# Decays two units ahead, rows one unit ahead, and TensorE in order of emission in the last image

## The chip, the cores and the metric

One core of one Trainium2 chip runs the whole program in one launch. The metric is device time in microseconds, and lower is better. The notes speak of the engines by the profile's names: PE is TensorE (PEld its weight loads), DVE is VectorE, ACT is ScalarE, POOL is GpSimd and SP is SyncE, which here only issues DMAs.

## The reference

The input is four images of 128 x 128 pixels and 128 channels, float32. Two residual layers follow each other, each behind a group norm:

```
x = x + deformable_conv(group_norm(x))      # layer 0: learned offsets, bilinear samples, 3x3 depthwise, pointwise
x = x + mamba(group_norm(x))                # layer 1: two blocks, each row of an image is a sequence of 128 steps
```

A mamba block projects each row to 256 channels `u` and 256 gates, runs a short causal convolution and SiLU on `u`, derives a step size `delta = softplus(...)` and 16 pairs of `B` and `C` per time step, and then runs, for each of the 256 channels and 16 states,

```
h[t] = exp(delta[t] * A) * h[t-1] + delta[t] * u[t] * B[t];   y[t] = sum over states of h[t] * C[t]
```

The sum, plus `u * D`, is gated with SiLU and projected back to 128 channels.

## The kernel before

**Two layers side by side.** `layer0(b)` is a generator over the 288 sampling steps of image `b`: POOL gathers table rows by indirect DMA (L370), DVE or ACT weights them (`gw`, L398 and L393), PE transposes and adds them (`p`) and multiplies with the weights (`acc`, L427). `layer1` is a generator over the mamba work. Image 0 passes layer 0 alone. After that, `layer0(b + 1)` and the mamba blocks of image `b` are stepped against each other, and the last image has the mamba work alone.

**Jobs and units.** A job is a block of four rows and one of the two mamba blocks: 64 jobs an image, 256 in all, ordered in pairs of blocks, so that the next job never needs this job's output. A job has eight units (`q` from 0 to 7) of two states each (`NQ = 2`). In the first three images a unit is:

- the decays: a small copy (L655) and four `Exp` on ACT (L660) into one of three buffers `da` (`NDA = 3`);
- the rows of `B` and `C`, spread over the partitions by DMA (`bc`, L650);
- on DVE two products `hs = du * B` (L694), one long scan (L700) and the product with `C` (L703);
- the sums: 16 transposing matmuls on PE that add `da` to `y` (through the helper, L137).

In the last image (`in_last`) `B` is multiplied in before a transpose. `turn_du` turns `du` on PE (`pdu`, L531) and ACT copies it (`duts`, L532). A unit's scans then take their input from PSUM: POOL (first state, L679) and ACT (second state, L677) scale `duts` to `xs`, PE transposes `xs` to four tiles `px` (16 transposes, L684), DVE runs four scans of 512 steps (L686) and one product (L689). The `px` tiles of each state share two PSUM buffers, so a transpose for the next unit can start when the scan of this unit that used the same buffer is done.

**The projections of the next job.** `pre` is a generator that is stepped once after each unit of the running job: `pu` (L554), SiLU (L564), gates `pr` (L569), `pdb` (L578) and the transposes `pbt` (L588), `pdt` (L600), the softplus on ACT (L603 to L615, with `Exp` and `Ln` from different function tables), and then `delta`: in the first three images summed on PE (`pdl`, L621) and copied by ACT (`de`, L622), in the last image on DVE (`e`, `de`, L611 to L613). The product `du` (L624) closes it. At a job's end DVE gates `y` (`g`, L710), PE transposes it (`pyg`, L715), ACT copies (`yg`, L716), PE projects (`pout`, L720 or L727 and L729), and the next job opens `y` with 8 matmuls against the diagonal of `D` (L639).

**What sets the order.** A list scheduler orders each engine's instructions when the program is built: whatever it holds ready goes out, the one emitted earlier first, by its own idea of the durations. On the chip each engine works its list from the top, so the list is fixed before the run. In the kernel before, a unit emits in this order: rows, decays, `xs` and `px`, scans, product, sums; then the piece of `pre`.

Of the kernel before, what the change touches and what calls it, by code (L numbers as in the profile page):

```python
# [10 lines left out]
F32 = mybir.dt.float32  # L11
I32 = mybir.dt.int32
AF = mybir.ActivationFunctionType
ALU = mybir.AluOpType
# [3 lines left out]
P = 128  # L18
# [46 lines left out]
def block_kernel(ctx: ExitStack, tc: tile.TileContext, a: dict, out: bass.AP):  # L65
# [69 lines left out]
    def add_transposed(o, v, start, stop):  # L135

        nc.tensor.matmul(o, v, ident, is_transpose=True, start=start, stop=stop, skip_group_check=True)  # L137
# [375 lines left out]
    def in_last(blk):  # L513

        return blk * SR // H == B - 1
# [19 lines left out]
    def pre(st, l):  # L535
# [68 lines left out]
            nc.scalar.activation(de[:, c], pdt, AF.Relu)  # L604
        nc.scalar.activation(e, e, AF.Exp, scale=-1.0)
        nc.scalar.activation(w1, e, AF.Identity, bias=1.0)
        nc.scalar.activation(du, w1, AF.Ln)
        if in_last(blk):
            nc.scalar.activation(w1, w1, AF.Identity, bias=-1.0)
            yield  # L610
            nc.vector.tensor_tensor(e, w1, e, ALU.subtract)  # L611
            nc.vector.tensor_tensor(de, de, e, ALU.subtract)
            nc.vector.tensor_tensor(de, de, du, ALU.add)  # L613
        else:
            nc.scalar.activation(w1, w1, AF.Identity, scale=-1.0, bias=1.0)  # L615
            yield
            yield
            for c in range(NC):
                pdl = now["ps1"].tile([P, TB], F32, tag="t", name=f"pdl_{nm}_{c}")
                for k, v in enumerate((e, w1, du, de)):  # L620
                    nc.tensor.matmul(pdl, ident, v[:, c], start=(k == 0), stop=(k == 3))  # L621
                nc.scalar.copy(de[:, c], pdl)  # L622
            yield
        nc.vector.tensor_tensor(du, de, u, ALU.mult)  # L624
        st.update(u=u, g=g, delta=de, du=du, bcd=bcd)
# [2 lines left out]
            yield  # L628
            turn_du(st, nm)

    def main(st, l):

        blk = st["blk"]
        nm = f"{blk}_{l}"

        y = now["psy"].tile([P, SR, NC, P], F32, tag="y", name=f"y_{nm}")
        for i in range(SR):
            for c in range(NC):
                nc.tensor.matmul(  # L639
                    y[:, i, c], st["u"][:, c, i * P : (i + 1) * P], ddiag[:, l, c, :],  # L640
                    start=(i % 2 == 0 and c == 0), stop=False, skip_group_check=True,
                )
        if in_last(blk) and "dut" not in st:
            turn_du(st, nm)
        for q in range(NS // NQ):
            bc = []
            for w in range(in_last(blk), 2):
                t = lm[0].tile([P, NQ, TB], F32, tag=f"bc{w}", name=f"bc{w}_{nm}_{q}", bufs=2)
                n0 = w * NS + q * NQ
                nc.sync.dma_start(t, st["bcd"][n0 : n0 + NQ, :].partition_broadcast(P))  # L650
                bc.append(t)
            da = das[n_da[0] % NDA]
            n_da[0] += 1

            nc.scalar.copy(da.rearrange("p c n s t -> p (c n s) t")[:, :, 0], zero)  # L655
            for c in range(NC):
                dv = st["delta"][:, c].rearrange("p (s t) -> p s t", s=SR)
                for n in range(NQ):
                    s = q * NQ + n
                    nc.scalar.activation(  # L660
                        da[:, c, n, :, 1:], dv[:, :, 1:], AF.Exp, scale=aneg[:, l, c, s : s + 1]
                    )
            dc = da.rearrange("p c n s t -> p c (n s t)")
            cv = bc[-1].rearrange("p n t -> p (n t)").unsqueeze(1).to_broadcast([P, NC, NQ * TB])
            if in_last(blk):


                for n in range(NQ):
                    s = q * NQ + n

                    xs = lm[0].tile(
                        [P, SR, NC * P], F32, tag="bc0" if n else "gw", name=f"xs_{nm}_{s}", bufs=2
                    )
                    for i in range(SR):
                        bv = st["bt"][:, i, s : s + 1]
                        if n:
                            nc.scalar.activation(xs[:, i], st["dut"][:, i], AF.Copy, scale=bv)  # L677
                        else:
                            nc.gpsimd.tensor_scalar(xs[:, i], st["dut"][:, i], bv, None, ALU.mult)  # L679
                    for c in range(NC):  # L680
                        pool, tag = (now["ps"], "t") if n else (psa, "acc")
                        px = pool.tile([P, SR, P], F32, tag=tag, name=f"px_{nm}_{s}_{c}")
                        for i in range(SR):
                            nc.tensor.transpose(px[:, i, :], xs[:, i, c * P : (c + 1) * P], ident)  # L684
                        dn = da[:, c, n].rearrange("p s t -> p (s t)")
                        nc.vector.tensor_tensor_scan(  # L686
                            dn, dn, px.rearrange("p s t -> p (s t)"), 0.0, ALU.mult, ALU.add
                        )
                nc.vector.tensor_tensor(dc, dc, cv, ALU.mult)  # L689
            else:  # L690
                hs = lm[0].tile([P, NC, NQ, TB], F32, tag="hs", name=f"hs_{nm}_{q}")

                for n in range(NQ):
                    nc.vector.scalar_tensor_tensor(  # L694
                        hs[:, :, n, :], st["du"], one,
                        bc[0][:, n].unsqueeze(1).to_broadcast([P, NC, TB]),
                        op0=ALU.mult, op1=ALU.mult,
                    )
                df = da.rearrange("p c n s t -> p (c n s t)")
                nc.vector.tensor_tensor_scan(  # L700
                    df, df, hs.rearrange("p c n t -> p (c n t)"), 0.0, ALU.mult, ALU.add
                )
                nc.vector.scalar_tensor_tensor(dc, dc, one, cv, op0=ALU.mult, op1=ALU.mult)  # L703
            for c in range(NC):
                for n in range(NQ):
                    for i in range(SR):
                        add_transposed(y[:, i, c], da[:, c, n, i, :], False, q == NS // NQ - 1 and n == NQ - 1)
            yield
        gt = st["g"]
        nc.vector.tensor_tensor(gt, y.rearrange("p s c d -> p s (c d)"), gt, ALU.mult)  # L710
        yg = lm[0].tile([P, NC, TB], F32, tag="yg", name=f"yg_{nm}")
        for c in range(NC):
            pt = now["ps1"].tile([P, SR, P], F32, tag="t", name=f"pyg_{nm}_{c}")
            for i in range(SR):
                nc.tensor.transpose(pt[:, i, :], gt[:, i, c * P : (c + 1) * P], ident)  # L715
            nc.scalar.copy(yg[:, c], pt.rearrange("p s t -> p (s t)"))  # L716
        po = now["ps1"].tile([P, TB], F32, tag="t", name=f"pout_{nm}")
        if l < NL - 1:
            for c in range(NC):
                nc.tensor.matmul(po, ow[:, l, c, :], yg[:, c], start=(c == 0), stop=(c == NC - 1))  # L720
            st["h"] = next_h()
            nc.scalar.copy(st["h"][:, :, DCONV - 1 :], po.rearrange("p (s t) -> p s t", s=SR))
        else:
            x1t = load_x1(blk, f"o{nm}")
            for i in range(SR):
                o = po[:, i * P : (i + 1) * P]
                nc.tensor.matmul(o, x1t[:, i * P : (i + 1) * P], ident, start=True, stop=False)  # L727
                for c in range(NC):
                    nc.tensor.matmul(  # L729
                        o, yg[:, c, i * P : (i + 1) * P], ow[:, l, c, :], start=False, stop=(c == NC - 1)  # L730
                    )
            ot = lm[0].tile([P, NC, TB], F32, tag="w1", name=f"ot_{nm}")[:, 0].rearrange("p (r c) -> p r c", r=SR)
            nc.scalar.copy(ot.rearrange("p r c -> p (r c)"), po)
            b, row = divmod(blk * SR, H)
            nc.sync.dma_start(out[b, row : row + SR].rearrange("r w c -> w r c"), ot)
# [4 lines left out]
    for i in range(0, NB, 2):  # L740
        sts = [{"blk": blk} for blk in range(i, min(i + 2, NB))]
        jobs += [(st, l) for l in range(NL) for st in sts]

    def layer1():
        open_main()
        for _ in pre(*jobs[0]):
            pass
        for i, job in enumerate(jobs):

            nxt = pre(*jobs[i + 1]) if i + 1 < len(jobs) else iter(())  # L750
            for _ in main(*job):
                next(nxt, None)
                yield
            for _ in nxt:
                pass

    for j in range(NJ):
        stats_part(0, j)
# [98 lines left out]
```

## Time and profile before

| | |
|---|---|
| median of three runs | 24469.56 us (24467.03 to 24477.43) |
| the profiled execution: its time, its span | 24467.72 us, 24465.9 us |
| granted TensorE clock, mean | 0.928 |
| busy over the span: PE, DVE, ACT, POOL | 84%, 84%, 65%, 74% |
| stretch 5000 to 19500 us: DVE, PE, ACT, POOL busy of 14500 us | 13598, 12719, 10324, 11689 us |
| stretch 20149 to 24450 us: DVE, PE, ACT, POOL busy of 4301 us | 3801, 3441, 3461, 2345 us |

The span falls into three parts: layer 0 of the first image alone (to about 3100 us), the three images in which both layers run side by side (to about 20100 us), and the last image, whose 64 jobs run from the first scan at 20149 us to the last at 24450 us. A profile row of a group has the line, the engine, the operation, what it writes and reads, the shape and the count; then the busy time, the mean of one, and the idle time of the engine just before these instructions with what ended it. A row of the waits has the time in total, how often, and the longest.

### The profile page before, as it was taken

What the parts mean: (1) busy time and instruction counts of PE and PEld (TensorE: products, weight loads), DVE (VectorE), ACT (ScalarE), POOL (GpSimd) and SP (SyncE); (2) the same over time, 40 slices, a digit from 0 to 9 for tenths busy, and PEclk for the clock granted to TensorE, in tenths of its full rate; (3) what the DMA queues carried; (4) which work ended last, traced back from release to release, by engine and by line L of the source; (5) the groups of instructions that cost most, each with busy time, mean ns of one, the idle gap of its engine ahead of it and who ended that gap; (6) DMA issues with size and microseconds to landing.
All of it is one profiled execution on the core that took longest, in us unless ns stands there. A gap on an engine that the chain in (4) does not pass through costs nothing. (4 is left out here: it accounts for less than half of the span.)

```text
span 24465.9 us, 304806 instructions
## 1 busy us (share of the span) xinstructions
PE 20571.8 (84%) x109348; PEld 12814.4 (52%) x109348; DVE 20647.2 (84%) x12769; ACT 15875.8 (65%) x36074; POOL 18054.1 (74%) x11270
## 2 busy tenths in 40 slices
PE   5777788888888888888888888888988878777777
PEld 3444445555555555555555555555555546666666
DVE  3332369999999999999999999999999998888888
ACT  1111147777777767777777766777777768888887
POOL 4777778888888857888888857888888845555555
PEclk7888889999999999999999999999999989999999
DMA  5554544554545544554555544455545532222221
GB/s 150 155 157 125 149 132 160 162 162 163 163 161 165 162 148 161 162 162 162 162 164 163 163 148 159 163 161 163 164 162 164 162 126 69 70 70 70 69 70 68
DMA packets 1530702, 3470.14 MB, mean 142 GB/s; under 512 B 243283, under 2 KB 717651, under 8 KB 1529052
## 3 DMA queue, kind: packets, MB, share of 16 engines
q1 hardware_dynamic: 1086812, 2242.08, 28.5%
q0 software_dynamic: 442368, 1208.55, 15.5%
q8 instruction: 859, 14.07, 0.2%
q14 instruction: 663, 5.43, 0.1%
HBM read 3299.19 MB, written 150.47 MB: 141 GB/s over the span
## 5 line engine op out<-in xcount | busy, mean ns | idle before, releaser
L370 POOL DMA_INDIRECT gt<-table,idx x9216 | 15702.9, 1704 | 4130.4 <-issue 2793.6
L700 DVE TENSOR_TENSOR_SCAN da<-da,hs 128x2048 f32<-128x2048 f32 x1536 | 6792.7, 4422 | 810.7 <-ACT da L660 708.2
L660 ACT ACTIVATE da<-de,aneg 128x508 f32<-128x508 f32 x8192 | 5450.1, 711 | 1447.6 <-PE y L137 1313.8
L427 PE MATMUL acc<-s,wc 128*64 128x512 f32 (+2 forms) x23520 | 5854.9, 609 | 143.0 <-ACT s L416 136.1
L137 PE MATMUL y<-ident,da 128*128 128x128 f32 x32768 | 4410.3, 291 | 1187.1 <-DVE da L703 911.6
L137 PEld LDWEIGHTS y<-ident,da 128*128 128x128 f32 x32768 | 3936.2, 150 | 2099.3 <-DVE da L703 1028.3
L679 POOL TENSOR_SCALAR xs<-duts,bt 128x256 f32<-128x256 f32 x2048 | 2350.4, 1164 | 2249.6 <-ACT duts L532 1190.4
L694 DVE SCALAR_TENSOR_TENSOR hs<-du,misc,bc 128x1024 f32<-128x1024 f32 x3072 | 3829.4, 1283 | 0.2
L137 PE MATMUL p<-ident,gw 128*128 128x128 f32 x18432 | 2592.6, 293 | 1375.2 <-DVE gw L398 1359.0
L427 PEld LDWEIGHTS acc<-s,wc 128*64 128x64 f32 (+1 forms) x23520 | 1940.7, 141 | 3368.5 <-issue 2999.7
L703 DVE SCALAR_TENSOR_TENSOR da<-da,misc,bc 128x2048 f32<-128x2048 f32 x1536 | 3609.3, 2350 | 39.0
L398 DVE TENSOR_TENSOR gw<-gt,wt 128x1024 f32<-128x1024 f32 x1440 | 1756.1, 1220 | 2219.3 <-DMA gt<-table,idx 2010.2
L393 ACT ACTIVATE gw<-gt,wt 128x64 f32<-128x64 f32 x13824 | 3487.9, 337 | 93.0 <-DMA gt<-table,idx 86.0
L137 PEld LDWEIGHTS p<-ident,gw 128*128 128x128 f32 x18432 | 2247.6, 151 | 1972.1 <-DVE gw L398 1513.7
L686 DVE TENSOR_TENSOR_SCAN da<-da,px 128x512 f32<-128x512 f32 x2048 | 2350.4, 1202 | 506.6 <-PE px L684 506.6
L416 ACT COPY s<-p 128x512 f32<-128x512 f32 x1152 | 671.3, 583 | 2332.7 <-PE p L137 2330.6
L554 PE MATMUL pu<-hp,inc 128*128 128x512 f32 x4096 | 1823.0, 593 | 0.2 <-ACT duts L532 0.2
L684 PE MATMUL px<-ident,xs 128*128 128x128 f32 x8192 | 1210.6, 287 | 542.9 <-DVE da L686 328.2
L684 PEld LDWEIGHTS px<-ident,xs 128*128 128x128 f32 x8192 | 968.5, 147 | 824.1 <-POOL xs L679 331.0
L413 ACT COPY s<-halo 128x256 f32<-128x256 f32 x1116 | 433.4, 401 | 1220.4 <-PE acc L427 1218.4
L689 DVE TENSOR_TENSOR da<-da,bc 128x2048 f32<-128x2048 f32 x512 | 1172.2, 2290 | 6.5
L554 PEld LDWEIGHTS pu<-hp,inc 128*128 128x128 f32 x4096 | 746.9, 189 | 821.1 <-issue 820.4
(148 smaller groups left out, 17815.0 us busy)
## 6 DMA issues: line engine op xcount, KB each, us to landing
bc<-bcd SPq DMA_DIRECT2D x3584, 512.0 KB
gt<-table,idx POOLq DMA_INDIRECT x9216
table<-xg SPq DMA_DIRECT2D x1016, 64.0 KB
xt<-in_x SPq DMA_DIRECT2D x124, 320.0 KB
xr<-in_x SPq DMA_DIRECT2D x128, 256.0 KB
x<-xo SPq DMA_DIRECT2D x128, 256.0 KB
x1t<-x SPq DMA_DIRECT2D x128, 256.0 KB
x1t_o<-x SPq DMA_DIRECT2D x128, 256.0 KB
```

The lines of the kernel that those rows point to most:

```text
L137: nc.tensor.matmul(o, v, ident, is_transpose=True, start=start, stop=stop, skip_group_check=True)
L370: nc.gpsimd.indirect_dma_start(out=gt[:, v, r], out_offset=None, in_=flat, in_offset=bass.IndirectOffsetOnAxis(ap=idx[:, ri, o : o + 1], a ...
L393: nc.scalar.activation(gw[:, r, s, v], gts[h][:, v, r, s * CG : (s + 1) * CG], AF.Copy, scale=wt[:, u, r0 + r, s, v : v + 1],)
L427: nc.tensor.matmul(accs[b, j][CG * g : CG * g + CG, q, :], wc[sl, v, e, :], st[p + 4 * g if p < 4 else 8][sl, ky + q.start : ky + q.stop, ...
L554: nc.tensor.matmul(px.rearrange("p (s t) -> p s t", s=SR), inc[:, l, j, c * P : (c + 1) * P], h[:, :, j : j + P], start=(j == 0), stop=(j ...
L660: nc.scalar.activation(da[:, c, n, :, 1:], dv[:, :, 1:], AF.Exp, scale=aneg[:, l, c, s : s + 1])
L679: nc.gpsimd.tensor_scalar(xs[:, i], st["dut"][:, i], bv, None, ALU.mult)
L684: nc.tensor.transpose(px[:, i, :], xs[:, i, c * P : (c + 1) * P], ident)
L686: nc.vector.tensor_tensor_scan(dn, dn, px.rearrange("p s t -> p (s t)"), 0.0, ALU.mult, ALU.add)
L694: nc.vector.scalar_tensor_tensor(hs[:, :, n, :], st["du"], one, bc[0][:, n].unsqueeze(1).to_broadcast([P, NC, TB]), op0=ALU.mult, op1=ALU. ...
L700: nc.vector.tensor_tensor_scan(df, df, hs.rearrange("p c n t -> p (c n t)"), 0.0, ALU.mult, ALU.add)
L703: nc.vector.scalar_tensor_tensor(dc, dc, one, cv, op0=ALU.mult, op1=ALU.mult)
```

## The change

The decays leave the unit: a new function `decays` takes the next entry of a list `queue` of all units of all jobs. Two entries are made before the first unit, and each unit emits, behind its own product, the decays of the unit two later. A new function `head` emits the rows, the `xs` and the `px` of a unit; it is called one unit ahead, in between the decays and the sums. For the last unit of a job the rest of `pre` and the head of the next job's first unit take this place (`after`). In the first three images the softplus gets one more stop ahead of `Ln`, and `delta` is published as soon as it is copied. From the first job of the last image on, PE's instructions are kept in the order of emission (`manual_schedule`); the other engines stay with the scheduler.

```
         nc.scalar.activation(w1, e, AF.Identity, bias=1.0)
+        if not in_last(blk):
+            yield
         nc.scalar.activation(du, w1, AF.Ln)
...
                 nc.scalar.copy(de[:, c], pdl)
+            st["delta"] = de
             yield
...
+    def decays(st, l, q):
+        da = das[n_da[0] % NDA]
+        n_da[0] += 1
+        nc.scalar.copy(da.rearrange("p c n s t -> p (c n s) t")[:, :, 0], zero)
...
+        made.append(da)
+
+    def head(st, l, q):
...
+        return bc, pxs
+
+    def main(st, l, first, after):
...
+        ahead = first
         for q in range(NS // NQ):
+            bc, pxs = ahead
+            da = made.pop(0)
...
+            last = q == NS // NQ - 1
+            for f in queue[:1]:
+                decays(*queue.pop(0))
+            ahead = after() if last else head(st, l, q + 1)
             for c in range(NC):
                 for n in range(NQ):
                     for i in range(SR):
-                        add_transposed(y[:, i, c], da[:, c, n, i, :], False, q == NS // NQ - 1 and n == NQ - 1)
-            yield
+                        add_transposed(y[:, i, c], da[:, c, n, i, :], False, last and n == NQ - 1)
+            if not last:
+                yield
         gt = st["g"]
...
+    queue = [(st, l, q) for st, l in jobs for q in range(NS // NQ)]
+    made = []
     def layer1():
         open_main()
         for _ in pre(*jobs[0]):
             pass
+        for _ in range(NDA - 1):
+            decays(*queue.pop(0))
+        firsts = {0: head(*jobs[0], 0)}
         for i, job in enumerate(jobs):
+            if i and in_last(job[0]["blk"]) and not in_last(jobs[i - 1][0]["blk"]):
+                ctx.enter_context(tc.manual_schedule(engines={mybir.EngineType.PE}))
             nxt = pre(*jobs[i + 1]) if i + 1 < len(jobs) else iter(())
-            for _ in main(*job):
+            def after(i=i, nxt=nxt):
+                for _ in nxt:
+                    pass
+                if i + 1 < len(jobs):
+                    firsts[i + 1] = head(*jobs[i + 1], 0)
+            for _ in main(*job, firsts.pop(i), after):
                 next(nxt, None)
                 yield
-            for _ in nxt:
-                pass
+            yield
```

More of the change, by code (lines that the diff above doesn't have):

```diff
@@ L629, in pre @@
             turn_du(st, nm)
-    def main(st, l):
+    def decays(st, l, q):
+        da = das[n_da[0] % NDA]
+        n_da[0] += 1
+        nc.scalar.copy(da.rearrange("p c n s t -> p (c n s) t")[:, :, 0], zero)
+        for c in range(NC):
+            dv = st["delta"][:, c].rearrange("p (s t) -> p s t", s=SR)
+            for n in range(NQ):
+                s = q * NQ + n
+                nc.scalar.activation(
+                    da[:, c, n, :, 1:], dv[:, :, 1:], AF.Exp, scale=aneg[:, l, c, s : s + 1]
+                )
+        made.append(da)
+    def head(st, l, q):
+        blk = st["blk"]
+        nm = f"{blk}_{l}"
+        if in_last(blk) and "dut" not in st:
+            turn_du(st, nm)
+        bc = []
+        for w in range(in_last(blk), 2):
+            t = lm[0].tile([P, NQ, TB], F32, tag=f"bc{w}", name=f"bc{w}_{nm}_{q}", bufs=2)
+            n0 = w * NS + q * NQ
+            nc.sync.dma_start(t, st["bcd"][n0 : n0 + NQ, :].partition_broadcast(P))
+            bc.append(t)
+        pxs = {}
+        if in_last(blk):
+            for n in range(NQ):
+                s = q * NQ + n
+                xs = lm[0].tile(
+                    [P, SR, NC * P], F32, tag="bc0" if n else "gw", name=f"xs_{nm}_{s}", bufs=2
+                )
+                for i in range(SR):
+                    bv = st["bt"][:, i, s : s + 1]
+                    if n:
+                        nc.scalar.activation(xs[:, i], st["dut"][:, i], AF.Copy, scale=bv)
+                    else:
+                        nc.gpsimd.tensor_scalar(xs[:, i], st["dut"][:, i], bv, None, ALU.mult)
+                for c in range(NC):
+                    pool, tag = (now["ps"], "t") if n else (psa, "acc")
+                    px = pool.tile([P, SR, P], F32, tag=tag, name=f"px_{nm}_{s}_{c}")
+                    for i in range(SR):
+                        nc.tensor.transpose(px[:, i, :], xs[:, i, c * P : (c + 1) * P], ident)
+                    pxs[n, c] = px
+        return bc, pxs
+    def main(st, l, first, after):
         blk = st["blk"]
@@ L642, in main @@
                 )
-        if in_last(blk) and "dut" not in st:
-            turn_du(st, nm)
+        ahead = first
         for q in range(NS // NQ):
[L646 to L662, printed above, removed]
+            bc, pxs = ahead
+            da = made.pop(0)
             dc = da.rearrange("p c n s t -> p c (n s t)")
@@ L668, in main @@
                 for n in range(NQ):
[L669 to L679, printed above, removed]
                     for c in range(NC):
[L681 to L684, printed above, removed]
                         dn = da[:, c, n].rearrange("p s t -> p (s t)")
                         nc.vector.tensor_tensor_scan(
-                            dn, dn, px.rearrange("p s t -> p (s t)"), 0.0, ALU.mult, ALU.add
+                            dn, dn, pxs[n, c].rearrange("p s t -> p (s t)"), 0.0, ALU.mult, ALU.add
                         )
```

## The prediction

> **What bounds the kernel now.** I read the page first (the tenths of busy time, then the groups), then busy time by stage, then DVE's waits in the two stages that the change touches, then the timeline of one job of the last image. The page:
>
> ```profile
> DVE  3332369999999999999999999999999998888888
> ...
> L700 DVE TENSOR_TENSOR_SCAN da<-da,hs 128x2048 f32<-128x2048 f32 x1536 | 6792.7, 4422 | 810.7 <-ACT da L660 708.2
> ```
>
> DVE is at nine tenths or more while both layers run, and near it in the last image; its scans (L700) waited 708.2 us for decays. By stage (length, then busy time of PE, PEld, DVE, ACT, POOL):
>
> ```profile
> 5000.00:19500.00 14500.00, 12718.79 (x65682) 7585.34 (x65680) 13598.40 (x7273) 10324.29 (x25068) 11688.75 (x6044) 0.95 0.50 161
> 20149.00:24450.00 4301.00, 3441.46 (x21515) 2679.45 (x21513) 3801.08 (x2875) 3460.74 (x6192) 2345.20 (x2043) 0.94 0.21 70
> ```
>
> DVE is idle for 902 us in the first and 500 us in the second, so its idle time is what can be won. Its waits in the first stage (total, times, longest):
>
> ```profile
> DVE da L700 <- ACT da L660: 614.5, 135, 12.4
> DVE gw L398 <- DMA gt<-table,idx: 64.7, 18, 7.2
> ```
>
> And in the last image:
>
> ```profile
> DVE da L686 <- PE px L684: 506.6, 145, 13.4
> ```
>
> The waits for decays all lie at q = 4, 5 and 6, where ACT has the softplus, the sampling products and two table loads in its list. Of the 507 us in the last image 456 lie at one place, the second scan of q = 2. The timeline shows a job boundary there, and a chain to remember:
>
> ```profile
> 22109.08 1.20 DVE L710 TENSOR_TENSOR g<-y,g 128x1024 f32<-128x1024 f32 x1
> ...
> 22113.48 1.50 PE L639 MATMUL y<-ddiag,u 128*128 128x128 f32 x12
> ...
> 22116.57 3.60 PE L554 MATMUL pu<-hp,inc 128*128 128x512 f32 x8
> ...
> 22125.89 3.44 DVE L686 TENSOR_TENSOR_SCAN da<-da,px 128x512 f32<-128x512 f32 x3 [6.67 <-PE px L684]
> ```
>
> PE works through two `pu` of 3.6 us and two sets of sums, and only then the next `px`: 6.67 us of idle DVE, once a job. The second chain:
>
> ```profile
> 22160.02 1.20 DVE L624 TENSOR_TENSOR du<-de,u 128x1024 f32<-128x1024 f32 x1
> ...
> 22161.97 1.07 ACT L532 COPY duts<-pdu 128x512 f32<-128x512 f32 x2 [0.41 <-PE pdu L531]
> 22162.72 9.77 POOL L679 TENSOR_SCALAR xs<-duts,bt 128x256 f32<-128x256 f32 x8 [13.94 <-ACT duts L532]
> ...
> 22168.30 1.22 DVE L686 TENSOR_TENSOR_SCAN da<-da,px 128x512 f32<-128x512 f32 x1 [0.41 <-PE px L684]
> ```
>
> From the end of `du` (22161.22) to the next job's first scan there are 7.08 us, the median over all jobs. DVE has a product and four scans in between, so only 0.4 us show.
>
> **First three images: the decays.** I compared the two built lists. No work is added there, and the table loads stay at four a job. What changes is what stands in ACT's list between one unit's decays and the next. I summed it in rows of the page net of overlap (`Exp` 5450.1/8192 = 0.665 us, `gw` 3048/12082 = 0.25 us, a table load 1.283 us, and so on) for the 1440 units of jobs 9 to 188. Over two units the sum passes 26 us at 170 units before and at none after, and those 170 carry 635 of the 672 us that these scans waited. Between 22 and 26 us lie 101 units before with 32 us (0.31 us each), and 167 after: 52 us. Sorted instead by the sum over one unit, the same reckoning leaves 145 us, over three units 210. I take 150, so 520 us of waits go (bounds 460 and 610).
>
> What is late next: POOL. A gather started beside a scan (L700) took 4.05 us, beside L703 2.15 us, and otherwise 0.95 us (medians of 1231, 1476 and 3336), so DVE's idle time is also POOL's. POOL waited 974 us for `gw` buffers, of which 454 remain, so it keeps up on average; but DVE's 65 us of waits for gathers should grow. I bound that by 0 and 300 us and take 100, nearer the row of 65. [...]
>
> `du` moves from q = 6 or 7 to the very end of the job, behind `de` (L622), which now follows 6.6 us (at most 11.1) of ACT work after the last decays. The scan and product of q = 7 take 6.8 us and the decays run some 5 us ahead, which hides it; without that cover it costs up to 4 us in each of 192 jobs. Rows and their DMAs go out one unit earlier on SP; DVE shows no wait for `bc` now, so I count nothing. **Gain here: 520 − 100 = 420 us.**
>
> **Last image: what goes.** With PE in order of emission the `px` of the next unit stand ahead of the sums and of `pu`. The whole 506.6 us of waits go: 7.9 us a job.
>
> **Last image: what comes.** A job is now a fixed ring of lists, the same for 62 of its 64 jobs.
> (A) DVE's list puts `du` behind the last product, directly ahead of the next job's first scan. The 7.08 us chain stays and has no cover. Besides, ACT's list has all eight `Exp` of the next two units ahead of the `duts` copies: they can start when `de` is done, take 8 x 0.665 = 5.3 us and end about 1.9 us after `du`, where the copies started 1.2 us after it. So 7.8 us (7.1 to 8.5).
> (B) DVE's list is product, `g`, scan of q = 1; PE's is sums, `pyg`, `pout`, the eight `ddiag` matmuls, and only then the `px` of q = 1. Before, the last `ddiag` ended 4.95 us after `g` (first block) or 5.67 us (second, whose `pout` is longer), two of the eight already done ahead of `pout` (0.5 us); the four transposes take 0.6 us. DVE has nothing in between: 6.2 us (5.5 to 7.3). Before, `px` up to q = 2 stood ahead of `pyg`.
> (C) At q = 2 and 3 PE has 12 transposes (1.4), sums (1.97), `pu` (3.6) and four transposes (0.5), 7.5 us, against DVE's four scans and product of 6.83: 0.7 us twice, 1.4 (0 to 2).
> (D) The softplus now starts behind the sums of q = 4, a unit later than before. Added up along ACT's list it reaches L609 about 0.9 us after DVE wants `e` in q = 7, and `dbl` holds PE 0.5 us: 1.0 taken (0 to 3).
> That is 16.4 us (12.6 to 20.8) for the 7.9 that go: 8.5 us a job (4.7 to 12.9), over 63 jobs **535 us more** (300 to 810).
>
> ACT also switches tables twice more a job (`Exp` moves in between the SiLU of `u` and of the gates): 110 loads of 1.283 us, 141 us, within ACT's 840 idle us there. If a job's ring lost its slack, they would cost those 141. [...]
>
> **The sum.** Against the profiled execution's 24467.7 us: − 420 + 535 = + 115, so 24583 us. The median of the runs is 1.9 us above that execution: 24585 us.
>
> **Rivals.** (1) Faster: the decays' waits go down to the 100 us that the shorter sums allow and POOL's slack holds (− 570), while the last image has only its two bare chains, 7.1 + 5.5 − 7.9 = 4.7 us a job, + 300, or up to + 380: some 24200 to 24300 us, 24250. The point is the job time of the last image: before it is 4301/64 = 67.2 us, and the gain of 420 us is used up at 67.2 + 420/63 = 73.9 us; my sum has 75.7. For it: A and B are the larger part and each has a row. Against: ACT and PE have ends of their own to add (C, D). (2) POOL: the 300 us of gather waits come, and 460 go: − 160 + 535, 24845 us. For it: the 4.05 us gathers; against: 974 us of POOL's own waits. (3) The decays change nothing that counts: the scheduler had sent them up to the buffers' limit before (ACT waited 904.4 us for `y` ahead of L660 in the first stage), and the waits come back elsewhere: 0 + 535, 25005 us. Against it are the 170 long sums, of which none is left.
>
> **How the numbers follow.** A run of this kernel can be told from no change beyond 0.2%, 49 us. The forecast has 0.55 (of it 0.41 slower, 0.11 same, 0.03 faster, since its own range with C and D at their ends and 460 to 560 us won is about 24400 to 24740), rival 1 has 0.22 (0.18 faster, 0.03 same, 0.01 slower), rival 2 0.13 and rival 3 0.10, both slower. That is 0.21 faster, 0.14 same, 0.65 slower. Leaving out the lower half of rival 1 and nearly all of rival 3, the range is 24300 to 24860 us.
>
> **What would show it.** Right: L700's waits for L660 fall to some 150 us; in the last image L686 waits at the first scan of q = 0 (about 7.8 us) and of q = 1 (about 6), no longer at q = 2's second, and a job takes 74 to 77 us. Wrong: jobs under 73.9 us there, waits for `gt` of several hundred us, or waits of `du` for L622.

## The result, and the profile after

The changed kernel takes 24650.28 us (median of 4 runs, 24643.87 to 24651.14) against 24473.5 us before (4 runs, 24467.03 to 24483.42): a ratio of 1.0071, 95% interval 1.0055 to 1.0086. It is slower, by more than the 0.2% that can be told from no change. The profiled execution took 24651.14 us, its span 24649.4 us.

The page of the changed kernel. The long scan of the first three images is now L721 (L700 before), the scan of the last image L707 (L686), the `Exp` of the decays L644 (L660), `px` L681 (L684):

```profile
DVE  3332369999999999999999999999999987777777
...
L721 DVE TENSOR_TENSOR_SCAN da<-da,hs 128x2048 f32<-128x2048 f32 x1536 | 6792.0, 4422 | 341.0 <-ACT da L644 201.5
...
L707 DVE TENSOR_TENSOR_SCAN da<-da,px 128x512 f32<-128x512 f32 x2048 | 2342.5, 1201 | 998.8 <-PE px L681 988.7
```

The waits of the long scan for its decays went from 708.2 to 201.5 us. Against that the waits of the last image's scans for `px` went from 506.6 to 988.7 us, and in the tenths DVE's last slices stand at 7 where they stood at 8. The same two stages as before (length, then busy time of PE, PEld, DVE, ACT, POOL, granted PE clock, DMA share, GB/s); the last image starts earlier, so its window does too:

```profile
5000.00:19500.00 14500.00, 12942.73 (x66936) 7690.45 (x66936) 13899.69 (x7407) 10520.93 (x25565) 12006.01 (x6175) 0.95 0.51 165
19789.00:24634.00 4845.00, 3728.26 (x21581) 2968.98 (x21581) 3835.38 (x2876) 3605.23 (x6325) 2042.45 (x2043) 0.82 0.18 62
```

In the first stage DVE is idle for 600 us instead of 902; in the last image for 1010 instead of 500. The granted PE clock of the last image fell from 0.94 to 0.82, which comes back below.

The first scan of the last image starts at 19789.6 us (20148.8 before), 359 us sooner. Its last scan ends at 24633.8 us (24449.6 before). A job of the last image takes (24633.8 − 19789.6)/64 = 75.69 us, before 67.20. So the change won 359 us and lost 64 x 8.49 = 543.

DVE's waits in the first stage (total, times, longest):

```profile
DVE da L721 <- ACT da L644: 190.5, 95, 5.9
DVE gw L398 <- DMA gt<-table,idx: 114.9, 40, 6.2
DVE loc L285 <- PE po L280: 45.2, 16, 5.8
DVE gw L398 <- PE p L137: 36.8, 14, 5.7
DVE du L627 <- ACT de L624: 26.3, 34, 2.4
DVE da L721 <- PE y L137: 25.7, 9, 4.0
```

The first row has fallen from 614.5; the row of the gathers has grown from 64.7, and the last two were hardly there.

In the last image the waits lie at two places of the job. The first, at the scan of q = 1, is the chain from the gate of the old job (timeline: start, length, engine and line, and in brackets the idle time ahead and what ended it):

```profile
21999.24 1.21 DVE L736 TENSOR_TENSOR g<-y,g 128x1024 f32<-128x1024 f32 x1
22000.51 1.92 PE L741 MATMUL pyg<-ident,g 128*128 128x128 f32 x8 [2.70 <-DVE g L736]
22002.25 2.85 PE L746 MATMUL pout<-yg,w_ow 128*128 128x512 f32 x4
22004.93 1.95 PE L693 MATMUL y<-ddiag,u 128*128 128x128 f32 x16
22006.71 1.91 PE L681 MATMUL px<-ident,xs 128*128 128x128 f32 x16
22007.42 4.55 DVE L707 TENSOR_TENSOR_SCAN da<-da,px 128x512 f32<-128x512 f32 x4 [6.97 <-PE px L681]
```

Everything that PE has for the end of a job stands ahead of the `px` that DVE waits for: 6.97 us in this job, 7.66 us on average over all. The second, at the first scan of a job, is the chain from `du`:

```profile
22058.49 1.22 DVE L627 TENSOR_TENSOR du<-de,u 128x1024 f32<-128x1024 f32 x1
22059.76 1.97 PE L531 MATMUL pdu<-ident,du 128*128 128x128 f32 x8 [6.89 <-DVE du L627]
22061.30 1.06 ACT L532 COPY duts<-pdu 128x512 f32<-128x512 f32 x2
22062.02 12.83 POOL L676 TENSOR_SCALAR xs<-duts,bt 128x256 f32<-128x256 f32 x12 [23.32 <-ACT duts L532]
22067.18 4.55 DVE L707 TENSOR_TENSOR_SCAN da<-da,px 128x512 f32<-128x512 f32 x4 [7.47 <-PE px L681]
```

DVE's list has nothing between `du` and that scan: 7.47 us here, 7.44 on average. Together the two places hold 15.1 of the 15.8 us that DVE stands idle in a job (1010/64; before 500/64 = 7.8).

### The profile page after: what moved, and what is told of

Same layout as the page of the kernel before. It is cut to its first block, busy times and chain, and to the rows that moved or that the text cites. A ratio compares the mean times of both kernels' runs of the same rounds, so it can differ in the third digit from the quotient of the medians.

```text
span 24649.4 us, 305073 instructions
## 1 busy us (share of the span) xinstructions
PE 20806.1 (84%) x109348; PEld 13032.2 (53%) x109348; DVE 20707.5 (84%) x12769; ACT 15993.1 (65%) x36184; POOL 17848.9 (72%) x11270
## 4 chain that ended last, share of the span: by engine, by line
PE 25%; POOL 24%; issue 18%; DVE 17%; ACT 12%; DMA 4%; SPq 0%; DVEq 0%; POOLq 0%; ACTq 0%
POOL gt L370 23%; PE acc L427 5%; ACT da L644 5%; DVE da L721 5%; DMA gt<-table,idx 4%; PE y L137 4%; PE pu L554 3%; DVE hs L715 3%; DVE da L707 2%; DVE da L724 2%; PE px L681 2%; ACT gw L393 1%; PE pdl L623 1%; PE y L693 1%; PE p L137 1%
## 5 line engine op out<-in xcount | busy, mean ns | idle before, releaser
L721 DVE TENSOR_TENSOR_SCAN da<-da,hs 128x2048 f32<-128x2048 f32 x1536 | 6792.0, 4422 | 341.0 <-ACT da L644 201.5
L644 ACT ACTIVATE da<-de,aneg 128x508 f32<-128x508 f32 x8192 | 5480.7, 712 | 1223.8 <-PE y L137 1124.2
L676 POOL TENSOR_SCALAR xs<-duts,bt 128x256 f32<-128x256 f32 x2048 | 2048.5, 1021 | 3055.2 <-ACT duts L532 1767.7
L137 PE MATMUL p<-ident,gw 128*128 128x128 f32 x18432 | 2718.3, 291 | 1283.3 <-DVE gw L398 1148.5
L707 DVE TENSOR_TENSOR_SCAN da<-da,px 128x512 f32<-128x512 f32 x2048 | 2342.5, 1201 | 998.8 <-PE px L681 988.7
L681 PE MATMUL px<-ident,xs 128*128 128x128 f32 x8192 | 1303.7, 307 | 440.2 <-POOL xs L676 225.4
L681 PEld LDWEIGHTS px<-ident,xs 128*128 128x128 f32 x8192 | 1051.3, 156 | 735.8 <-POOL xs L676 307.4
L741 PE MATMUL pyg<-ident,g 128*128 128x128 f32 x2048 | 426.3, 376 | 850.4 <-DVE g L736 850.3
```

Of the source, the lines that this page charges most:

```text
L644: nc.scalar.activation(da[:, c, n, :, 1:], dv[:, :, 1:], AF.Exp, scale=aneg[:, l, c, s : s + 1])
L707: nc.vector.tensor_tensor_scan(dn, dn, pxs[n, c].rearrange("p s t -> p (s t)"), 0.0, ALU.mult, ALU.add)
L721: nc.vector.tensor_tensor_scan(df, df, hs.rearrange("p c n t -> p (c n t)"), 0.0, ALU.mult, ALU.add)
```

## Experiments: the first three images

Theory: the decays two units ahead take the waits away, because no stretch of ACT work between two units' decays is long enough any more to empty the buffers. Rivals: the extra stop ahead of `Ln` does it, or the rows ahead.

**e5_no_stop**, the change without the stop:

```
         nc.scalar.activation(w1, e, AF.Identity, bias=1.0)
-        if not in_last(blk):
-            yield
         nc.scalar.activation(du, w1, AF.Ln)
```

> The changed kernel without the extra stop ahead of the logarithms (so the work ahead still runs a unit earlier, and the decays are still emitted two units ahead). Summed from the row durations, stretches of ACT work between two units' decays that are longer than 26 us occur 170 times in the profile of before, never in that of the change, and 43 times in the order of this kernel. Theory (the decays two units ahead clear most of the long stretches and the stop the rest): waits of the scans for their decays go from the change's 200 us to about 300, the last image starts near 19,880 us (19,790 in the change), the job of the last image stays at 75.7 us: 24,740 us, a ratio to before of 1.011. Rival (the stop is the whole gain of the first three images): waits near 700 us, last image from 20,150, 25,010 us.

Measured: 24786.94 us (4 runs), ratio 1.0127 (1.011 to 1.0144); last image from 19931.4 us, 75.65 us a job. The page's scan row:

```profile
L719 DVE TENSOR_TENSOR_SCAN da<-da,hs 128x2048 f32<-128x2048 f32 x1536 | 6792.6, 4422 | 494.1 <-ACT da L642 346.8
```

Of the 507 us that the change takes from these waits, 361 (708.2 − 346.8) come without the stop and 145 with it. The stop is the smaller part, as the theory said, though somewhat larger than the 100 expected.

**e6_decays_own**, the change with the decays of the first three images in their own unit:

```
         for q in range(NS // NQ):
             bc, pxs = ahead
+            if not made:
+                decays(*queue.pop(0))
             da = made.pop(0)
...
-            for f in queue[:1]:
+            while in_last(blk) and queue and len(made) < NDA - 1:
                 decays(*queue.pop(0))
```

> The changed kernel, but in the first three images the decays are emitted in their own unit as before; rows a unit ahead, the stop, and the whole last image stay as in the change. Stretches of ACT work over 26 us: 161, as good as the 170 of before. Theory (it is the decays' place that makes the gain of the first three images): waits for decays 650 to 700 us, last image from about 20,150 us, its job at 75.7 us, so 25,000 us, ratio 1.021. Rival (the rows ahead or the stop make the gain): last image from 19,790 us and 24,650 us.

Measured: 25063.54 us (2 runs), ratio 1.0241 (1.0221 to 1.0262); last image from 20208.6 us, 75.63 us a job.

```profile
L723 DVE TENSOR_TENSOR_SCAN da<-da,hs 128x2048 f32<-128x2048 f32 x1536 | 6791.2, 4421 | 802.3 <-ACT da L644 701.7
```

The waits are those of before, with the rows a unit ahead and the stop both in place. So without the decays two units ahead these two, together, make no gain.

**e7_before_stop**, the kernel before with the two lines of the stop (the lines that e5 takes out):

> The kernel before with nothing but the extra stop ahead of the logarithms. Stretches of ACT work over 26 us: 161 (170 without it). Theory (the stop by itself does not clear the long stretches): the time of before, 24,470 us, within 60 us either way, waits for decays near 680 us. Rival (the stop makes the gain of the first three images): 24,110 us.

Measured: 24526.88 us (10 runs), ratio 1.0022 (1.0012 to 1.0032); last image from 20204.9 us, the waits 688.0 us. The stop alone takes 20 us from these waits and costs 47 us of time; DVE's waits for gathers in the first stage are 108.5 us there (64.7 before). The stop is worth its 145 us only where the decays are two units ahead. The three runs fit sums over ACT's list of the kind that the prediction made: stretches above 26 us number 170, 161, 161, 43 and 0 in the kernel before, e7, e6, e5 and the change, and the waits are 708, 688, 702, 347 and 202 us, in the same order but for the two that have 161. The five traces give nearly the same counts: ACT's busy time from the end of one unit's `Exp` to the end of those two units later is above 24 us at 170, 163, 163, 44 and 3 units of the same jobs.

## Experiments: the last image

Theory: the job's 8.5 us come from two bare chains, (A) from `du` to the next job's first scan, because the work ahead is stepped too late, and (B) from the gate to the `px` of q = 1, because PE's list puts the end of a job ahead of them. Rival: keeping PE in order costs all of it.

**e1_free_pe**, the change with PE left to the scheduler:

```
-            if i and in_last(job[0]["blk"]) and not in_last(jobs[i - 1][0]["blk"]):
-                ctx.enter_context(tc.manual_schedule(engines={mybir.EngineType.PE}))
```

> The changed kernel with PE given back to the scheduler in the last image; decays, heads and the stop ahead of Ln stay. Theory (the loss of the last image is PE's order: du behind the last product, px behind the projection of the output): the scheduler now puts du ahead of a product and four of unit 7's operations, and the px of q = 1 ahead of the output's projection. A (7.4 us a job) goes but for 0.5 to 1, B (7.7) shrinks to some 4 in two pieces (the last px of q = 1 stand behind the projection: 2.3; pu behind them: 1.5), so a job takes about 65 us, and the program about 23,970 us. Rival (the loss comes from emitting the heads a unit ahead: late softplus, 110 more table loads, ACT's list; whatever PE's order): a job stays near 75 us and the program near 24,650 us.

Measured: 24367.21 us (4 runs), ratio 0.9956 (0.9939 to 0.9972), 71.37 us a job. That is neither the one number nor the other. DVE's waits from 20300 to 24100 us:

```profile
DVE da L707 <- PE px L681: 314.0, 215, 4.8
DVE da L707 <- ACT da L639: 257.7, 51, 5.1
```

The wait at the first scan of q = 1 is gone; what is left for `px` is spread over the job. At the first scan of a job there is still a wait, 5.04 us on average, which the rows put down to the decays' small copy (L639). Its timeline:

```profile
22041.68 1.20 DVE L627 TENSOR_TENSOR du<-de,u 128x1024 f32<-128x1024 f32 x1
...
22050.49 0.47 PE L681 MATMUL px<-ident,xs 128*128 128x128 f32 x1 [2.98 <-POOL xs L676]
22050.76 3.62 PE L137 MATMUL y<-ident,da 128*128 128x128 f32 x16
...
22054.17 1.70 PE L681 MATMUL px<-ident,xs 128*128 128x128 f32 x11
...
22054.70 4.55 DVE L707 TENSOR_TENSOR_SCAN da<-da,px 128x512 f32<-128x512 f32 x4 [5.05 <-ACT da L639]
```

Here `du` comes a product, two scans and another product (6.8 us) ahead of that scan, where the change has nothing. But PE stands for a late `xs`, then works through the 16 sums of an older unit, and only then through 11 of the 16 `px`, one of which the first scan needs. ACT's copy waits for the same sums, which end at 22054.38, and the scan starts 0.3 us after them: both things that it can have waited for stand behind these sums. So giving PE back to the scheduler takes off 4.3 of the 8.5 us a job (75.69 − 71.37). It moves `du` as well, so this run doesn't part the two chains; e2 and e3 do.

**e2_tail_later**: `g`, `pyg`, `pout` and the opening of the next `y` are put in a function and called behind the transposes for q = 1 of the next job; PE still in order.

```
+        y = None if tails else open_y()
...
             ahead = after() if last else head(st, l, q + 1)
+            if y is None:
+                tails.pop()()
+                y = open_y()
...
+        if in_last(blk) and queue_left(st, l):
+            tails.append(tail)
```

> The changed kernel; in the last image the end of a job (gate, pyg, output projection) and the opening of the next y are emitted behind the head of the next job's second unit, so PE has the px of q = 1 ahead of them. PE stays in order of emission. Theory: the 7.7 us wait at the first scan of q = 1 goes. What stands behind it on PE is now pyg, pout, the opening of y, the sums and pu, 11.2 to 11.9 us after g, against 6.8 us of scans and product: 4.4 to 5.1 us of wait come at the first scan of q = 2. A stays at 7.4. A job takes about 72.7 us, the program about 24,460 us. Rival (B is caused by something that the order of these instructions doesn't touch): 75.7 us a job, 24,650 us. On the clock: if PE's half clock follows its idle time, pout takes 1.9 us again instead of 3.2, since PE is busy ahead of it.

Measured: 24433.4 us (8 runs), ratio 0.9981 (0.9971 to 0.9991), 72.38 us a job. The wait at q = 1 is 0.06 us a job, a wait of 4.65 us stands at q = 2 instead, and A stays at 7.44. B was the place of these pieces; moved back by a unit, the chain still does not fit in one unit of 6.9 us.

**e3_du_earlier**: the work ahead gets one step more after q = 2, so that `du` comes a unit earlier.

```
-            for _ in main(*job, firsts.pop(i), after):
+            for k, _ in enumerate(main(*job, firsts.pop(i), after)):
                 next(nxt, None)
+                if k == 2 and in_last(job[0]["blk"]):
+                    next(nxt, None)
```

> The changed kernel; in the last image the projections are stepped twice after q = 2 (gates and B, C, dt in one piece), so the softplus, du and its transposes come a unit earlier. Theory: du now has a product, four scans and a product of cover, and A (7.4 us at q = 0) goes but for 0.5; g moves ahead of the product of q = 0, which covers 2.3 of B: 5.4 left; the double piece makes PE late at q = 4 by some 2.5 us. About 68.4 us a job, 24,180 us. Rival (A is ACT's and POOL's own slowness, not the place of du): the wait at q = 0 stays at 7 us and the program above 24,550 us.

Measured: 24364.04 us (3 runs), ratio 0.9954 (0.9938 to 0.997), 71.48 us a job. A is down to 0.08 us and the wait at q = 1 to 5.53, both as expected. At q = 4 a wait of 5.28 us came up where 2.5 were expected: two steps now stand behind one unit, and PE's list has `pdb` and `pbt`, which wait for ACT (131.4 and 46.5 us over 53 jobs), ahead of the `px` of q = 4.

**e4_both**, e2 and e3 together:

> Both edits of the last two runs, PE in order of emission. Theory: A gone, of B some 2.4 us left at the first scan of q = 2, 2.5 us at q = 4: about 65.4 us a job, 23,990 us. If the waits only move from place to place with PE's list in order (rival), a job stays above 70 us, 24,290 us.

Measured: 24167.0 us (2 runs), ratio 0.9874 (0.9854 to 0.9893), 68.13 us a job: faster than both kernels. It is not the 65.4 us that the sum of both edits promised. Left are 2.21 us at q = 2 and 5.27 us at q = 4. What PE waited for, from 20300 to 24100 us:

```profile
PE px L681 <- ACT xs L674: 328.6, 56, 6.7
PE pdb L578 <- ACT g L574: 140.4, 56, 3.6
```

Both are once a job, and both are waits for ACT. The second lies in unit 3 with the `px` of q = 4 behind it, and DVE pays for it: an engine that works in order passes a late piece on to the transposes behind it. The first is longer, but it lies in unit 6, ahead of the `px` of q = 7, and DVE waits only 0.12 us a job there.

## Experiments: two versions meant to do better

**e8_steps_mid**: e2, and the pieces of the work ahead called between a unit's transposes and its sums (q = 1, 2, 4, 6), and behind the sums of q = 2, 3 and 4.

```
+            def mid(q, nxt=nxt, late=late):
+                if late and q in (1, 2, 4, 6):
+                    next(nxt, None)
+            for k, _ in enumerate(main(*job, firsts.pop(i), after, mid)):
+                if not late or k in (2, 3, 4):
+                    next(nxt, None)
```

> The changed kernel with the end of each job of the last image (gate, transposes, projection, and the opening of the next sum) emitted behind the transposes for the next job's second unit, as in the earlier run of that alone, and with the pieces of the work ahead emitted between a unit's transposes and its sums (units 1, 2, 4, 6) and behind the sums of units 2, 3 and 4, which puts the next job's scaled inputs a unit earlier. TensorE still runs in order of emission. Theory: the wait for the next job's first scan (7.4 us a job) falls to 0 to 1 as in the run with the scaled inputs earlier; the wait at the third unit, 4.65 us in the run with the end emitted later, loses the 1.4 us of the piece of projection that stood ahead of it: 3.2 us; nothing new at units 4 and 5, where the run with the end later had none. Job 59.9 + 3.2 + 0.5 + 1 = 64.6 us, ratio 0.978, 23,930 us. Rival (the stalls only move, as they did to the fifth unit when both edits were run with the pieces at their old places): 67 us or more a job, 24,100 us or more.

Measured: 24324.24 us (4 runs), ratio 0.9938 (0.9922 to 0.9955), 70.86 us a job. The two predicted terms came (3.06 us at q = 2, 0.08 at q = 0), and the rival came with them: 1.94 us at q = 4, 0.97 at q = 5, and a wait that was not there before (DVE's waits, 20300 to 24100 us):

```profile
DVE da L711 <- PE px L681: 345.8, 175, 4.1
DVE e L613 <- ACT w L611: 196.0, 53, 4.5
```

DVE's list now has the subtraction `e` in q = 6 before ACT has made `w`, and the scans behind it stand for 3.69 us a job.

**e9_thirds**: the last image's blocks in threes, one piece to each unit, and PE, ACT and DVE all in order of emission.

```
-                ctx.enter_context(tc.manual_schedule(engines={mybir.EngineType.PE}))
+                ctx.enter_context(tc.manual_schedule(engines={mybir.EngineType.PE, mybir.EngineType.Activation, mybir.EngineType.DVE}))
...
+    for i in range((B - 1) * n1, NB, 3):
+        sts = [{"blk": blk} for blk in range(i, min(i + 3, NB))]
...
+    STEPS = {0: 1, 1: 1, 2: 1, 3: 1, 4: 1, 5: 1, 6: 1, 7: 0}
```

> A version drawn from the earlier runs. The first three images are those of the change (decays two units ahead, rows one, the stop), but for the load of x1, which lands in the tile of the projected input and is scaled there. In the last image the blocks go through the two layers in threes instead of pairs, so that the work ahead of a job no longer waits for the job just ended; TensorE, ACT and VectorE all run in the order of emission, and that order puts one piece behind the transposes of each unit: projection with the gate of the job before (unit 0), its transposes (1), the projection of the row parameters (2), softplus (3 and 4), gate product and scaled input (5), transposed scaled input and output projection (6). Table loads in the whole program fall from 1287 to 1159. Theory (the waits of the last image are set by where pieces stand in the queues, not by an engine's load): both chains of the change's job have a unit or more of cover, VectorE waits 1 to 3 us a job beside its 59.9 us of work; 62 us a job, 64 jobs from 19,790 us: 23,775 us, ratio 0.971. Rival (ACT, with some 54 us of work a job and every piece in order, becomes the bound and the stalls move again, as in the run with the pieces at their middle places): 66 us or more a job, 24,030 us or more.

Measured: 24581.96 us (4 runs), ratio 1.0045 (1.0028 to 1.0061), 74.66 us a job: the rival, and worse than it said. ACT's waits from 20300 to 24100 us, 51 jobs:

```profile
ACT u L566 <- PE y L719: 212.2, 51, 4.9
ACT dbl L588 <- PE pdb L585: 206.8, 51, 5.0
ACT yg L759 <- PE pyg L758: 135.9, 51, 2.7
```

The first three alone are 10.9 us a job in which ACT stands in its list for a piece that PE has not reached, with the scaled inputs and decays of the next units behind it. ACT is busy for 3424 us of 4761 there, so its load is not the bound; the order written by hand is. DVE is idle for 14.0 us a job, spread over many places. Whether a better order for three engines exists was not tried on the chip. e4, with PE alone in order, is the fastest version found.

## Why the prediction was right

The time, 24650.28 us, lies in the range, on the side that was thought likelier and 65 us above the forecast of 24585. The branch was the forecast's, and the break-even of 73.9 us a job was passed by 1.8. By its steps, against the profiled execution:

- **First three images: 420 forecast, 359 came.** The waits for decays fell by 507 (520 forecast), and to 202 us where 150 were named. The term given back was too small: from 3100 us to the last image, DVE's waits for gathers grew by 45 us (230.4 to 275.8) where 100 were allowed, but three waits that the prediction counted at nothing or did not name came up: `loc` for PE +37 (13.7 to 50.4), `du` for `de` +25 (20.2 to 45.4), the scan for `y` +28 (0 to 28.4). The cover that was named for `du`, the scan and product of q = 7, did not hold 34 times in the stretch from 5000 to 19500 us. DVE was also busy 30 us longer (15784 to 15814).
- **What goes, 7.9 us a job:** right. No wait is left at q = 2's second scan.
- **A, 7.8 us (7.1 to 8.5):** 7.44. Named rightly and in its bounds: the `duts` copies started 1.6 us after `du`, behind the eight `Exp` (1.9 forecast, 1.2 before). e3 took it away by making `du` earlier.
- **B, 6.2 us (5.5 to 7.3):** 7.66, above its bounds. The chain was right, as e2 showed by moving it. Its size was not: the term was built from rows of before, where the granted PE clock was 1.00 in such a chain (22110 to 22114 us); in the change the chain from 22000.5 us ran at 0.53, then 0.50, up to 22004.0 us (last section).
- **C, 1.4 us (0 to 2), and D, 1.0 us (0 to 3):** about 0.1 and 0.4. A unit with `pu` took 6.93 us against 6.83 of DVE's own work, not 7.5. The forecast added the durations of PE's rows, but consecutive rows overlap: `px`, sums and `pu` have 1.91, 1.91 and 3.60 us, and the next `px` starts 6.93 us after the first (22013.65 and 22020.58 us). For D, DVE never waited for `e`; the 0.4 us stand at the first scan of q = 6, for `px`.
- **The sum of the last image:** +543 us for +535 forecast, 75.69 us a job for 75.7. This agreement is partly luck. B was 1.5 us too small, A, C and D together 2.3 too large, and DVE's busy time rose by 0.5 us a job (59.39 to 59.93), which the forecast did not have.
- **Table loads:** 110 more, as counted (1177 to 1287); ACT still had 1240 us of idle time in the last image, and DVE's waits there are for `px` but for 4.2 us, so nothing speaks for a cost.
- **The rivals:** the faster one took the two chains bare (7.1 and 5.5 us) and 570 us won; the chains came at 7.4 and 7.7 us, and 507 less 148 given back. POOL's 300 us of gather waits did not come: DVE's idle time fell by 302 us in the first stage, and its gather waits rose by 50 there.
- **The range:** its upper part is a little short. With A and B as forecast, C and D at their ends and 460 to 560 us of waits gone, the prediction's own terms give about 24395 to 24810 us, not 24400 to 24740; the measured time lies in both.

## What to carry to other kernels

Issuing the input of a scan two units ahead paid here because the engine that makes it had stretches of other work longer than the buffers cover; count the stretches in its list, since their number went with the waits of five kernels (170 stretches and 708 us before, none and 202 us in the change). Keeping an engine in order of emission fixes which wait comes last, and every piece that it waits for holds up all that stands behind (in e9 ACT stood 10.9 us a job for three pieces, in e4 DVE 5.27 us behind `pdb`): find for each such piece a unit in which its inputs are there already, and look at what the piece behind it serves. A chain's price taken from rows of a busy engine can be too low if the change lets that engine stand before the chain: here `pout` took 955 ns a matmul behind a stand of 2.70 us, and 608 ns in the rows of before. When a row names what ended a wait, look in the timeline at everything that ends then, and ask of a long wait of another engine whether the engine that sets the pace pays for it.

## What the runs showed of the hardware

In the changed kernel PE's granted clock was half just after PE had stood for 2.70 us, and the chain that ended the stand ran at that clock. Windows around the two chains (length, busy times, then the granted clock, DMA share and GB/s); the first holds the stand itself:

```profile
21997.20:22000.50 3.30, 0.61 (x6) 0.37 (x4) 3.25 (x2) 2.78 (x8) 2.91 (x1) 1.00 0.03 7
22002.00:22004.00 2.00, 2.00 (x4) 0.86 (x4) 0.00 (x0) 0.78 (x2) 0.00 (x0) 0.50 0.05 20
22005.00:22007.00 2.00, 2.00 (x20) 2.00 (x19) 0.00 (x0) 0.59 (x1) 0.00 (x0) 1.00 0.00 0
...
22059.70:22062.00 2.30, 1.97 (x8) 1.57 (x8) 0.01 (x1) 2.30 (x5) 0.00 (x0) 0.50 0.62 216
```

`pyg` ran at 0.53 (22000.5 to 22002.0 us) and `pout` at 0.50 up to 22004.0 us; by the `ddiag` matmuls of 22005 us the clock was full again. The eight `pyg` took 1.92 us, before 1.09; from the start of `pout` to the first `ddiag` passed 2.68 us, before 1.77. That is 1.7 us, a little more than what B has over its forecast. Over all jobs the last `ddiag` ended 6.75 us after `g` in first blocks and 7.52 in second ones, where it had ended 4.95 and 5.7 before. The groups show that it is not this job alone (PE, 20300 to 24100 us; the number behind the comma is the mean of one matmul in ns), first the changed kernel, then the kernel before, then e4:

```profile
L746 PE MATMUL pout<-yg,w_ow 128*128 128x512 f32 x96 | 77.9, 955 | 0.0
```

```profile
L720 PE MATMUL pout<-yg,w_ow 128*128 128x512 f32 x112 | 54.4, 608 | 0.1
```

```profile
L754 PE MATMUL pout<-yg,w_ow 128*128 128x512 f32 x112 | 55.5, 618 | 6.7 <-ACT yg L750 6.7
```

The same matmul took 955 ns where PE had stood 2.70 us ahead of the chain, and 618 ns in e4, where it came without such a stand (ahead of `pyg` PE stood 23.6 us in all there, 140.5 in the change); in e2 it took 633 ns (20200 to 24200 us), as its expectation had foretold. The granted clock of the last image goes with it: 0.94 before, 0.82 in the change, 0.86 in e2, 0.91 in e4. No run changed the clock alone, so the 1.5 us are worked out and not shown by themselves.

The clock was full again at 22004.0 us, 3.5 us after `pyg` started: it was 0.50 from 22003.5 to 22004.0 us and 0.98 from 22004.0 to 22004.5 us. The stand of 2.70 us came ahead of the half clock: from 21997.2 to 22000.5 us, which holds it, the clock was at 1.00. A half clock does not always follow a stand of such a length. In the kernel before, two stands of 2.42 us ended at 22105.54 and 22172.54 us; the clock was 1.00 from 22105.0 to 22108.2 us after the one, and 0.50 from 22173.2 to 22176.5 us after the other. What decides between the two, no run shows.
